# A graph attention layer on one core: the second part's instruction order written by hand, the last tile by column halves, one slot more summed on TensorE

## The chip, the cores and the metric

The kernel runs on one core of a Trainium2 chip. Its engines have queues of their own and meet through semaphores: TensorE (PE, matmuls; its weight loads are listed as PEld), VectorE (DVE), ScalarE (ACT), GpSimd (POOL) and SyncE (SP). SyncE and GpSimd issue the DMAs. The metric is the device time of one execution in microseconds (us). The kernel before was run nine times: median 1314.67 us, from 1309.21 to 1318.92.

## What is computed

`x` is 3327 x 1024 in fp32, `adj` a symmetric 0/1 matrix of 3327 x 3327 with ones on the diagonal, in which a row has some 17 ones on average and 37 at most. The weights are 1024 x 1024. Cut to what matters:

```python
h = jnp.maximum(_layernorm(x), 0.0)
f = h @ Wf + bf
g = h @ Wg + bg
e = relu(f @ g.T)
attention = softmax(where(adj > 0, e, -9e15), axis=1)
out = x + attention @ (h @ W + bW)
```

Only entries with `adj > 0` count, so each row needs the scores of its neighbours alone: `f_i . g_j = (h_i A + v) . h_j + const`, with `A = Wf Wg^T`, and `sum_j p_ij (h_j W + bW) = (sum_j p_ij h_j) W + bW`.

## The kernel before, in words

**First part (to about 270 us; its code is not touched).** It normalises x, writes h to DRAM (`hd`), builds each row's list of neighbours (`pd`), sorts the rows by their number of neighbours, and computes A (`A_sb`). All engines run it in an order written by hand, inside `manual_schedule`.

**Second part.** The sorted rows are 26 tiles of 128. Tile s takes `CAPS[s]` neighbour slots (37, 25, 23 ... 11), and the tiles run in `ORDER`: 24, 15, then 0 to 14, 16 to 23, and 25. The text calls `CAPS[s]` the cap. For a slot k, GpSimd gathers 128 rows of h, one per partition, into a tile `G` (128 x 1024 fp32, 26 buffers). Per tile:

- `fetch`: GpSimd gathers the list `pi` and the tile's own rows `hp`, two tiles ahead. `turned` (L917) transposes `hp` on TensorE, `taken` (L924) copies it to `hT` on ScalarE.
- `third` (L936): q = h A + v in three column thirds, 16 matmuls each, on TensorE, into two banks `ps_q` that ScalarE has filled with v. `emptied` (L946, and L884 by `filled`) copies a third to `q` on ScalarE and fills the bank again. The q of a tile is made two tiles ahead: thirds 0 and 1 behind the earlier tile's combine, the last third inside `project`, and its copy at the next unit's softmax (the list `late`).
- `dot` (L986): a score per slot, one DVE pass over G and q. All three thirds of q must be there.
- `softmax` (L995 to L1011): mask and maximum on DVE (`nm`), the exp on ScalarE (L1002) with its sum l, and, for a second chunk, the correction `al` (L1005) and the scaling of y by it (L1011).
- `combine`: y = sum of p_k G_k. Slot 0 is scaled on ScalarE and becomes y (L1050); the others are either a DVE pass (L1052, "sum" below), or, for the slots that `on_tensor` picks, scaled on ScalarE (L1046) and added on TensorE as 8 transposes that accumulate in PSUM (L1026, `yT_ps`). A slot on TensorE is called a slot on PE below, and m is their number.
- `project`: y itself is added into `yT_ps` the same way, ScalarE copies it to `yT` (L1060), and TensorE multiplies it by W (L1068, 32 matmuls).
- `result` (L1090, L882): ScalarE scales the product by 1/l and fills the banks again; GpSimd adds x by a gather. `finish` (L1102) writes the rows out. For the last tile DVE does it (L1084).

Tiles with more than 16 slots (0 to 14) are done in two chunks: the first of 10 slots (19 for tile 0), all summed on DVE, then the rest, of which m = min(cap - 12, slots - 2) go to TensorE. A one-chunk tile sends cap - 12 there; the two last tiles, 23 and 25, cap - 7; the first two half. A "unit" is a tile's chunk. Each unit of the main loop (L1147 to L1193) runs, in the order of the text: its dots, its softmax, the copy of a last third from `late`, up to three dots of the next unit (`AHEAD`), `finish`, `turned`, `combine`, and, behind a tile's last chunk, `result` of the tile before, `third` 0, its copy, `third` 1, and then `rest` (the copy of third 1, and `project`), which waits until behind the next unit's combine where the next unit is a first chunk.

**What sets the order.** In the second part the queues are not in the order of the text. A planner with a cost model places each engine's instructions. `in_line` chains some of them: the instructions made inside it come behind the last ones noted in `queue["pe"]` and `queue["act"]`. This holds the projections, the transposes, the copies, the exp and the last scaling of a tile in the text's order on TensorE and ScalarE; dots and sums on DVE are placed by the planner.

Of the kernel before, what the change touches and what calls it, by code (L numbers as in the profile page):

```python
# [33 lines left out]
AHEAD = 3  # L34
# [262 lines left out]
def edge_path(ctx: ExitStack, tc: tile.TileContext, x, adj, Wf, bf, Wg, bg, W, bW, out, flag):  # L297
# [563 lines left out]
    queue = {}  # L861

    @contextmanager
    def in_line():
        with ExitStack() as both:
            for ins in queue.values():
                both.enter_context(tc.issue_after(ins.ins))
            yield


# [15 lines left out]

    one = small.tile([P, 1], FP, name="one")
    tc.keep_in_program_order(nc.scalar.activation(one, ident[:, :1], AF.Exp))

    for at in range(2):  # L890
        filled(p_q, "ps_q", vb, QB, 6 + at, True)
        filled(p_o, "ps_o", bWb, CB, at, True)
# [15 lines left out]
    def turned(s):  # L908
        e = st[s]
        e["hT"] = hTpool.tile([P, KD, P], FP, name="hT")  # L910
        e["ps_t"] = []
        for g in range(0, KD, 4):
            ps = p_t.tile([P, 4, P], FP, name="ps_t")
            e["ps_t"].append(ps)
            with in_line():
                for k in range(4):
                    ins = nc.tensor.transpose(ps[:, k, :], e["hp"][:, (g + k) * P : (g + k + 1) * P], ident)  # L917
            queue["pe"] = ins

    def taken(s):  # L920
        e = st[s]
        for g, ps in enumerate(e["ps_t"]):
            with in_line():
                queue["act"] = nc.scalar.copy(e["hT"][:, 4 * g : 4 * g + 4, :], ps)  # L924

    def third(s, i):
# [7 lines left out]
        with in_line():  # L934
            for k in range(KD):
                ins = nc.tensor.matmul(  # L936
                    ps[:, :QB], e["hT"][:, k, :], A_sb[:, k, o : o + QB], start=False, stop=(k == KD - 1),
                    skip_group_check=True,
                )
        queue["pe"] = ins  # L940

    def emptied(s, i):
        e = st[s]
        at = 3 * ORDER.index(s) + i
        with in_line():
            ins = nc.scalar.copy(e["q"][:, i * QB : (i + 1) * QB], e["ps_q"][i][:, :QB])  # L946
            if at + 2 < 3 * NT:
                ins = filled(p_q, "ps_q", vb, QB, at + 2)
        queue["act"] = ins
# [27 lines left out]
    G = {}  # L977

    def dot(s, k, behind=None):
# [5 lines left out]
        with tc.issue_after(behind.ins) if behind else ExitStack():  # L985
            nc.vector.tensor_tensor_reduce(  # L986
                junk, g, e["q"][:, :D], 1.0, e["q"][:, D : D + 1], op0=ALU.mult, op1=ALU.add,
                accum_out=e["sc"][:, k : k + 1],
            )

    def softmax(s, k0, k1, last):
# [5 lines left out]
        nc.vector.tensor_reduce(nm, sc, AX.X, ALU.max, negate=True)  # L997
        if k0:
            nc.vector.tensor_tensor(nm, nm, e["nm"], op=ALU.min)  # L999
        l = small.tile([P, 1], FP, name="l")  # L1000
        with in_line():
            nc.scalar.activation(sc, sc, AF.Exp, bias=nm, accum_out=l)  # L1002
        if k0:
            al = small.tile([P, 1], FP, name="al")
            nc.scalar.activation(al, e["nm"], AF.Exp, bias=nm, scale=-1.0)  # L1005
            nc.vector.scalar_tensor_tensor(l, e["l"], al, l, op0=ALU.mult, op1=ALU.add)
        if last:
            e["rs"] = small.tile([P, 1], FP, name="rs")
            nc.vector.reciprocal(e["rs"], l)
        if k0:  # L1010
            queue["act"] = nc.scalar.activation(e["y"], e["y"], AF.Copy, scale=al)  # L1011
        e["nm"], e["l"] = nm, l

    def on_tensor(s, k0, k1):


        m = min(max(0, CAPS[s] - (7 if s in ORDER[-2:] else 12)), k1 - k0 - 2) if s not in ORDER[:2] else (k1 - k0) // 2
        ks = range(max(k0, 1), k1)
        return [k for i, k in enumerate(ks) if (i + 1) * m // len(ks) > i * m // len(ks)]

    def sum_transposed(e, g, first, last):
# [3 lines left out]
        for c in range(KD):  # L1025
            ins = nc.tensor.matmul(  # L1026
# [210 lines left out]
```

## Time and profile before

| what | value |
|---|---|
| median of 9 runs | 1314.67 us |
| profiled execution | 1314.56 us, span 1312.8 us |
| busy: PE, DVE, ACT, POOL | 1119.6, 1157.4, 609.9, 891.1 us |
| second part from 399 to 1246 us: PE, DVE | 786.9, 793.5 of 847 us |
| dots L986 | 468, 1284 ns each |
| sums L1052 | 275, 1285 ns each |
| scalings for TensorE L1046 | 167, 1142 ns each |
| gathers of G, bytes read over the span | 454; 284 GB/s read and written |

The span runs from the first to the last instruction of one profiled execution; the execution's own time is 1.8 us longer. Busy times are the union of an engine's instructions; matmuls are pipelined, so a busy PE is not at its peak. In a time line a row gives start and duration in us, engine, line, operation, output <- inputs, count, and in brackets how long the engine stood idle before it and what ended that. DVE instructions overlap at their ends: a sum of 1.28 us is followed by the next one 1.2 to 1.3 us after its start.

### The profile page before, as it was taken

The page shows a single profiled execution, that of the slowest core. Times are in us where ns is not written, and L with a number is a line of the kernel's source. Part 1 is how long each engine was busy: PE and PEld are TensorE (multiplying, and loading weights), DVE is VectorE, ACT ScalarE, POOL GpSimd, SP SyncE. Part 2 cuts the span into 40 slices and gives each one's busy share as a digit, 9 for nine tenths or more (in the row PEclk, how much of TensorE's full clock was granted, in tenths as well). Part 3 has the DMA queues.
Part 4 walks back from the last instruction along what each step waited for, and adds up shares of the span by engine and source line. Part 5 has one row for each costly group of instructions (what it writes and reads, how often), then busy time and mean ns, then how long its engine had stood idle before and what let it go on. Part 6 is the DMA issues. An engine that isn't in the chain of part 4 may idle for free.

```text
span 1312.8 us, 14316 instructions
## 1 busy us (share of the span) xinstructions
PE 1119.6 (85%) x4488; PEld 703.8 (54%) x4488; DVE 1157.4 (88%) x2205; ACT 609.9 (46%) x943; POOL 891.1 (68%) x678
## 2 busy tenths in 40 slices
PE   2799962958837999899889998999999899999995
PEld 2566641644615556556655655556555565555553
DVE  6999977687899888999999999999999999999990
ACT  5999976133207345435542454443345433333350
POOL 8999974375675777777667666776665666666611
PEclk9899985987878999899999999999999999999998
DMA  9999995787787998899888898888888788888821
GB/s 372 415 398 403 408 326 184 273 307 259 242 286 241 319 321 285 291 308 310 276 297 276 280 310 291 282 276 288 280 289 273 223 279 290 273 297 273 280 74 50
DMA packets 101802, 374.44 MB, mean 285 GB/s; under 512 B 14747, under 2 KB 18490, under 8 KB 98519
## 3 DMA queue, kind: packets, MB, share of 16 engines
q0 software_dynamic: 80624, 290.96, 66.7%
q1 hardware_dynamic: 21094, 82.49, 16.3%
q8 instruction: 37, 0.61, 0.2%
q14 instruction: 47, 0.39, 0.1%
HBM read 344.11 MB, written 29.30 MB: 284 GB/s over the span
## 4 chain that ended last, share of the span: by engine, by line
DVE 32%; issue 29%; DMA 14%; PE 9%; POOL 7%; ACT 5%; another core or an unknown queue 2%; SPq 0%; POOLq 0%; DVEq 0%; ACTq 0%
DVE G L1052 13%; DMA G<-hd,pi 8%; DVE cand L482 6%; POOL G L356 6%; DVE junk L986 6%; PE yT_ps L1026 4%; PE ps_o L1068 3%; DMA xt<-in_x_dram 3%; PE ps_q L936 2%; ACT G L1046 2%; DVE sc L986 1%; DMA A_sb<-in_L_gnn_Wg_dram 1%; DVE held L493 1%; DMA G<-hd,perm 1%
## 5 line engine op out<-in xcount | busy, mean ns | idle before, releaser
L356 POOL DMA_INDIRECT G<-hd,pi x454 | 535.6, 1180 | 198.5 <-issue 103.6
L986 DVE CUSTOM_DVE_ANT_0 junk<-G,q 128x1024 bf16<-128x1024 f32 x468 | 601.0, 1284 | 33.8 <-DMA G<-hd,pi 15.8
L1052 DVE SCALAR_TENSOR_TENSOR G<-G,sc 128x1024 f32<-128x1024 f32 x275 | 353.4, 1285 | 36.8 <-ACT G L1011 21.4
L1068 PE MATMUL ps_o<-W_sb,yT 128*128 128x512 f32 x832 | 363.8, 595 | 6.3 <-ACT yT L1060 6.3
L936 PE MATMUL ps_q<-A_sb,hT 128*128 128x342 f32 x1152 | 347.3, 455 | 9.6 <-issue 9.5
L936 PEld LDWEIGHTS ps_q<-A_sb,hT 128*128 128x128 f32 x1152 | 216.6, 191 | 119.0 <-issue 17.4
L1026 PE MATMUL yT_ps<-ident,G 128*128 128x128 f32 x1544 | 206.3, 285 | 85.8 <-ACT G L1046 65.4
L1068 PEld LDWEIGHTS ps_o<-W_sb,yT 128*128 128x128 f32 x832 | 157.5, 190 | 200.8 <-issue 188.0
L1026 PEld LDWEIGHTS yT_ps<-ident,G 128*128 128x128 f32 x1544 | 177.4, 146 | 118.1 <-ACT G L1046 80.8
L419 POOL TENSOR_TENSOR r<-r,iotaj 128x1664 f32<-128x1664 f32 (+3 forms) x50 | 183.7, 3712 | 12.2 <-ACT r L412 12.2
L1046 ACT ACTIVATE G<-G,sc 128x1024 f32<-128x1024 f32 x167 | 182.4, 1142 | 0.0
L1002 ACT ACTIVATE sc<-sc,nm 128x10 f32<-128x10 f32 (+11 forms) x41 | 12.5, 305 | 342.5 <-DVE nm L999 252.0
L552 PE MATMUL ps_A<-WgT,WfT 128*128 128x342 f32 x432 | 132.7, 466 | 2.1 <-ACT WfT L547 2.1
L482 DVE MAX8 cand<-r 128x8 f32<-128x208 f32 (+2 forms) x416 | 119.1, 360 | 4.0 <-POOL r L419 3.6
L552 PEld LDWEIGHTS ps_A<-WgT,WfT 128*128 128x128 f32 x432 | 82.9, 195 | 43.5 <-issue 3.9
L946 ACT COPY q<-ps_q 128x342 f32<-128x342 f32 x72 | 31.4, 436 | 158.7 <-PE ps_q L936 123.6
L412 ACT ACTIVATE r<-r 128x3327 f32<-128x3327 int32 (+3 forms) x27 | 77.3, 2863 | 7.8 <-DMA r<-in_adj_dram 7.8
L1102 POOL DMA_INDIRECT out_dram<-res,perm x25 | 32.1, 1284 | 68.1 <-DMA res<-in_x_dram,perm 66.2
L356 POOL DMA_INDIRECT res<-in_x_dram,perm x25 | 43.1, 1723 | 51.1 <-ACT res L1090 42.6
L924 ACT COPY hT<-ps_t 128x512 f32<-128x512 f32 x48 | 25.4, 580 | 75.6 <-PE ps_t L917 75.6
L356 POOL DMA_INDIRECT pi<-pd,perm x26 | 30.9, 1189 | 33.8 <-DMA cd<-cand 17.7
L536 PE MATMUL ps_tr<-ident,A_sb 128*128 128x128 f32 x128 | 23.0, 343 | 26.3 <-DMA A_sb<-in_L_gnn_Wg_dram 23.3
(139 smaller groups left out, 718.5 us busy)
## 6 DMA issues: line engine op xcount, KB each, us to landing
r<-in_adj_dram SPq DMA_DIRECT2D x24, 1663.5 KB, 12.0
xt<-in_x_dram SPq DMA_DIRECT2D x25, 512.0 KB, 12.7
hd<-xt SPq DMA_DIRECT2D x25, 512.0 KB, 10.5
G<-hd,pi POOLq DMA_INDIRECT x454
A_sb<-in_L_gnn_Wg_dram SPq DMA_DIRECT2D x8, 512.0 KB, 17.2
A_sb<-in_L_gnn_Wf_dram SPq DMA_DIRECT2D x8, 512.0 KB, 11.1
W_sb<-in_L_gnn_W_dram POOLq DMA_DIRECT2D x1, 4096.0 KB
cd<-cand SPq DMA_DIRECT2D x25, 64.0 KB, 11.8
```

What stands on the lines that cost most here:

```text
L356: return nc.gpsimd.indirect_dma_start(out=to, out_offset=None, in_=table, in_offset=bass.IndirectOffsetOnAxis(ap=idx, axis=0), **kw,)
L412: nc.scalar.activation(r[:n, b:e], a[:n, b:e], AF.Sign, accum_out=to)
L419: eng.tensor_mul(r[:n, b:e], r[:n, b:e], iotaj[:n, b:e])
L482: nc.vector.max(cands[t][:n, s * 8 : s * 8 + 8], r[:n, s * SW : min(N, (s + 1) * SW)])
L552: nc.tensor.matmul(ps[:, :QB], WfTs[c][:, k, :], WgT[:, k, o : o + QB], start=(k == 0), stop=(k == KD - 1))
L936: ins = nc.tensor.matmul(ps[:, :QB], e["hT"][:, k, :], A_sb[:, k, o : o + QB], start=False, stop=(k == KD - 1), skip_group_check=True,)
L986: nc.vector.tensor_tensor_reduce(junk, g, e["q"][:, :D], 1.0, e["q"][:, D : D + 1], op0=ALU.mult, op1=ALU.add, accum_out=e["sc"][:, k : k ...
L1026: ins = nc.tensor.matmul(e["yT"][:, c, :], g[:, c * P : (c + 1) * P], ident, is_transpose=True, start=(first and c % 4 == 0), stop=(last a ...
L1046: queue["act"] = nc.scalar.activation(g, g, AF.Copy, scale=p)
L1052: e["summed"] = nc.vector.scalar_tensor_tensor(y, g, p, y, op0=ALU.mult, op1=ALU.add)
L1068: ins = nc.tensor.matmul(ps, yT[:, k, :], W_sb[:, k, o * CB : (o + 1) * CB], start=False, stop=(k == KD - 1), skip_group_check=True,)
L1102: ins = nc.gpsimd.indirect_dma_start(out=out[:, :], out_offset=bass.IndirectOffsetOnAxis(ap=perm[:, s : s + 1] if s < N // P else final, a ...
```

## The change

1. The whole second part runs inside `manual_schedule` for ScalarE, VectorE and TensorE: these three take their instructions in the order of the text. `in_line`, `queue` and the other explicit order edges go. GpSimd and SyncE stay with the planner.
2. The text's order is new in places. `softmax` issues the correction `al` ahead of the exp, and the scaling of y right behind it; l and its inverse move to `totalled`, behind the dots that follow. `AHEAD` is 2 instead of 3, from the third unit on. `combine` calls `between` behind each DVE sum, which puts one dot of the next unit there (not in the last tile but one).
3. `on_tensor`: a second chunk of s slots sends min(cap - 11, s - 1) to TensorE instead of min(cap - 12, s - 2): one more in each of the 15 two-chunk tiles, so that DVE sums one slot there. Tile 23 sends 3 instead of 6, tile 25 sends 5 instead of 4.
4. The last tile (25) runs `ended` instead of `combine` and `project`: slot 0 is scaled on DVE, y is summed on DVE by column halves, and each half is transposed, copied and multiplied by its half of W's rows before the next. `result` of tile 23 stands ahead of it in the text.
5. The load of the flag that chooses the dense path moves to behind the last `finish` but one.

Cut to its core:

```diff
-AHEAD = 3
+AHEAD = 2
...
-    def softmax(s, k0, k1, last):
+    def softmax(s, k0, k1):
...
         if k0:
             nc.vector.tensor_tensor(nm, nm, e["nm"], op=ALU.min)
-        l = small.tile([P, 1], FP, name="l")
-        with in_line():
-            nc.scalar.activation(sc, sc, AF.Exp, bias=nm, accum_out=l)
+            e["al"] = small.tile([P, 1], FP, name="al")
+            nc.scalar.activation(e["al"], e["nm"], AF.Exp, bias=nm, scale=-1.0)
+        nc.scalar.activation(sc, sc, AF.Exp, bias=nm, accum_out=l)
         if k0:
-            al = small.tile([P, 1], FP, name="al")
-            nc.scalar.activation(al, e["nm"], AF.Exp, bias=nm, scale=-1.0)
-            nc.vector.scalar_tensor_tensor(l, e["l"], al, l, op0=ALU.mult, op1=ALU.add)
-        if last:
-            e["rs"] = small.tile([P, 1], FP, name="rs")
-            nc.vector.reciprocal(e["rs"], l)
-        if k0:
-            queue["act"] = nc.scalar.activation(e["y"], e["y"], AF.Copy, scale=al)
+            nc.scalar.activation(e["y"], e["y"], AF.Copy, scale=e["al"])
+        else:
+            e["y"] = G[s, 0]
+            if s != ORDER[-1]:
+                nc.scalar.activation(e["y"], e["y"], AF.Copy, scale=e["sc"][:, :1])
...
-        m = min(max(0, CAPS[s] - (7 if s in ORDER[-2:] else 12)), k1 - k0 - 2) if s not in ORDER[:2] else (k1 - k0) // 2
+        if s in ORDER[:2]:
+            m = (k1 - k0) // 2
+        elif s in ORDER[-2:]:
+            m = {ORDER[-2]: 3, ORDER[-1]: 5}[s]
+        else:
+            m = min(max(0, CAPS[s] - (11 if k0 else 12)), k1 - k0 - 1)
...
+                nc.vector.scalar_tensor_tensor(y, g, p, y, op0=ALU.mult, op1=ALU.add)
+                between()
+
+    def ended(s, k1):
...
+        for i, k in enumerate(pe):
+            nc.scalar.activation(G[s, k], G[s, k], AF.Copy, scale=e["sc"][:, k : k + 1])
+            for c in range(KD):
+                transposed_into(e, G[s, k], c, not i and c % 4 == 0, False)
+        for g in range(0, KD, 4):
+            half = slice(g * P, (g + 4) * P)
+            nc.vector.tensor_scalar(y[:, half], y[:, half], e["sc"][:, :1], None, op0=ALU.mult)
...
+            for c in range(g, g + 4):
+                transposed_into(e, y, c, False, c % 4 == 3)
+            nc.scalar.copy(yT[:, g : g + 4, :], e["yT"][:, g : g + 4, :])
+            for o, ps in enumerate(e["o"]):
+                for k in range(g, g + 4):
...
+    with tc.manual_schedule(engines={
+        mybir.EngineType.Activation, mybir.EngineType.DVE, mybir.EngineType.PE
+    }):
...
+            dots(s, range(k0, k1))
...
+            softmax(s, k0, k1)
+            if late:
+                emptied(late.pop(), 2)
+            covered = AHEAD if i > 1 else 0
+            dots(s2, range(a, min(b, a + covered)))
+            totalled(s, k0, last)
...
+            coming = iter(range(a + covered, b) if i > 1 and s != ORDER[-2] else ())
+
+            def between(s2=s2, coming=coming):
+                for k in coming:
+                    dots(s2, [k])
+                    break
+
+            if s == ORDER[-1]:
+                result(ORDER[at - 1])
+                ended(s, k1)
+                done_with.append(ORDER[at - 1])
+                break
+            combine(s, k0, k1, last, ahead, between)
+            if rest:
+                rest()
+                rest = None
+            if last:
+                if at:
+                    result(ORDER[at - 1])
+                    done_with.append(ORDER[at - 1])
+                if ahead is not None:
+                    third(ahead, 0)
+                    emptied(ahead, 0)
+                    third(ahead, 1)
...
+        finish(done_with.pop())
+        bad = nc.values_load(flag[0:1, 0:1], min_val=0, max_val=1 << 20)
+        result(ORDER[-1])
+        finish(ORDER[-1])
```

## The prediction, made before the result was known

> **What bounds the kernel now.** I read the windows by stage first, then VectorE's (DVE's) waits, then the time lines around three hand-overs. The second part runs from about 270 us to the end at 1312.8; from 399 us on it repeats one pattern per row tile, and at 1246 us a tail begins. The windows (columns: busy us of each engine, granted clock, DMA share, GB/s):
>
> ```profile
> core 0: us, PE busy (x) PEld busy (x) DVE busy (x) ACT busy (x) POOL busy (x), PEclk, DMA share, GB/s
> 399.00:1246.00 847.00, 786.89 (x3219) 493.12 (x3220) 793.49 (x1162) 360.99 (x575) 581.42 (x480) 0.99 0.86 285
> 1246.00:1313.00 67.00, 52.27 (x193) 28.27 (x191) 31.26 (x40) 20.96 (x29) 8.98 (x8) 0.92 0.23 64
> ```
>
> DVE has work for 793.5 of 847 us, so it sets the pace, with TensorE (PE) just behind. In the tail DVE has 31 us of 67: PE sets the end there. What DVE lacks in the 847 us is mostly ScalarE (ACT), in the list of its waits (us in total, times, longest):
>
> ```profile
> DVE G L1052 <- ACT G L1011: 21.4, 14, 1.7
> DVE G L1052 <- ACT G L1050: 9.3, 7, 3.1
> DVE l L1006 <- ACT al L1005: 5.8, 9, 0.7
> ```
>
> So 36 us could come back. Why these waits are small is seen where a tile's second chunk (18 slots of the first two-chunk tile, softmax ready at n = 398.97) hands over to the next tile's first chunk. ACT, then DVE:
>
> ```profile
> 417.79 1.16 ACT L1046 ACTIVATE G<-G,sc 128x1024 f32<-128x1024 f32 x1
> 418.85 0.68 ACT L1090 ACTIVATE res<-ps_o,rs 128x512 f32<-128x512 f32 x1
> ...
> 425.60 0.45 ACT L946 COPY q<-ps_q 128x342 f32<-128x342 f32 x1 [4.01 <-PE ps_q L936]
> 426.45 0.30 ACT L1002 ACTIVATE sc<-sc,nm 128x10 f32<-128x10 f32 x1
> 426.88 1.15 ACT L1050 ACTIVATE G<-G,sc 128x1024 f32<-128x1024 f32 x1
> ```
>
> ```profile
> 426.69 1.28 DVE L986 CUSTOM_DVE_ANT_0 junk<-G,q 128x1024 bf16<-128x1024 f32 x1
> 428.06 1.28 DVE L1052 SCALAR_TENSOR_TENSOR G<-G,sc 128x1024 f32<-128x1024 f32 x1
> ```
>
> The next chunk's scores were ready on DVE at 418.8, but its exp ran only at 426.45: ACT first scaled 16 slots for PE, then stood at the copy of q, which waits for PE. DVE lost nothing, because the planned order put seven more dot products (418.7 to 427.9) in front of the first weighted sum. That cover is what I look for in the new order.
>
> **The change, part by part.** Prices, start to start: a dot in a run 1.325 (425.37 to 426.69), a sum in a run 1.31 (three in 3.93), a sum and a dot alternating 2.405; a slot's scaling on ACT 1.05 (13 in 13.63); 8 transposes on PE 0.90 (56 matmuls in 6.28); a third of q 4.7 (two in 9.37); one output projection 13.9.
>
> (1) One slot more on PE in 15 two-chunk tiles: DVE loses one sum each, 1.2 us where it was paired, some 16 to 18 us in all. PE and ACT gain 0.9 and 1.05 each. On PE that is covered (a tile of cap 20 needs 3 x 4.7 + 13.9 + 1.0 + 10 x 0.9 + 0.7 = 38.7 there, below its 42 us); on ACT it lies in the chain above and delays the next exp. GpSimd's gathers stay with the planner: DVE waited 2.0 us for them in all, and a later DVE asks for them later: 0, bounds -2 and +3.
>
> (2) The order by hand, at the second chunk's softmax. It puts two dots of the next tile behind the softmax, as cover. They need that tile's q, whose last third is copied on ACT behind the correction, the exp and the scaling of y: 0.19 + 0.43 + 1.04 + 0.42 issue to issue in the rows at 399.0, so the dots start at n + 2.15. Today DVE lost 0.65 + 1.67 there in ten tiles and 1.2 in four. The cover covers nothing; gain 0.2 in ten, loss 1 in four.
>
> (3) At the next first chunk. From n DVE now does: wait 2.15, two dots 2.65, l and its inverse 0.35, the one sum and a dot 2.45, seven dots 9.3, softmax 0.4, two covering dots 2.65. That is n + 20.0; then the sum stands in the queue, and all later dots behind it. ACT: in three undisturbed tiles the copy of q began 9.02 + 1.05 m after n (19.52 at m = 10, 18.47 at m = 9 twice; m slots on PE), and copy to sum took 2.46 (425.60 to 428.06). So the sum starts at the later of n + 20.0 and n + 11.5 + 1.05 m. With the new m = 17, 14, 12, 11, 10, 10, 9, 9 this is 29.35, 26.2, 24.1, 23.05, 22, 22, 20.95, 20.95, and 20.0 for the other six. Fourteen hand-overs: 308.6. From there to the next second chunk's softmax: nine sums, paired while dots are left, and the rest, with 0.8 of small steps: 27.75, 25.1, 23.8, 22.45 twice, 21.35 twice, 20.25 twice, 19.15 twice, 18.05 three times (caps 25 to 17): 297.2. Together 605.8 against 587.8 today (exps at 399.00 and 986.83): **+18.0**. Counted the other way, as DVE work (10 sums; the pairs that are lost give back 0.235 each, net -9.5) plus waits (14 x 2.15 + 28.6 = 58.7 against 35.5), it is +13.7. I take +16.
>
> (4) Transition to one-chunk tiles. The softmax of the tile of cap 16 comes at n + 25.2 (2.15 + 2.65 + 0.35 + 2.45 + 13 dots 17.2 + 0.4) against 28.9: **-3.7**, since sums that now run there are gone or later.
>
> (5) One-chunk tiles. Here the last third of the next q is on PE behind the previous tile's y. Today's first such tile shows that chain:
>
> ```profile
> 1043.81 1.97 PE L1026 MATMUL yT_ps<-ident,G 128*128 128x128 f32 x8 [5.28 <-DVE G L1052]
> 1045.57 5.43 PE L936 MATMUL ps_q<-A_sb,hT 128*128 128x342 f32 x16
> 1051.04 0.44 ACT L946 COPY q<-ps_q 128x342 f32<-128x342 f32 x1 [0.59 <-PE ps_q L936]
> 1051.51 1.28 DVE L986 CUSTOM_DVE_ANT_0 junk<-G,q 128x1024 bf16<-128x1024 f32 x1 [0.51 <-ACT q L946]
> ```
>
> Today two sums ran at 1048.40 while q was late. In the new order two dots stand before the first sum, so a ring closes: q, 2 dots 2.65, inverse 0.2, 11 sums with a dot between 24.05 + 1.2, y on PE 0.9, third 4.7, copy 0.8 = 34.5 us per tile, whatever its cap. Today the seven periods from 1015.72 to 1245.69 sum to 230.0. New: first Q at n + 2.15, six rings 207.0, and 29.7 from the last Q to the softmax (28.1 to y, a dot 1.2, 0.4): 238.85, **+8.9**. Without the ring, caps 14 and 13 would take 33.2 and 31.9 and all but 1 us of it would go.
>
> (6) Tail. Three slots instead of six on PE in the tile before the last, but its nine sums follow two dots that wait for q (n + 4.8): y at n + 19.45, PE's projection ends at n + 36.2 (today 34.8). Then ACT's queue decides:
>
> ```profile
> 1270.93 4.25 ACT L1046 ACTIVATE G<-G,sc 128x1024 f32<-128x1024 f32 x4
> ...
> 1280.61 0.69 ACT L1090 ACTIVATE res<-ps_o,rs 128x512 f32<-128x512 f32 x1 [4.13 <-PE ps_o L1068]
> 1281.33 0.69 ACT L882 ACTIVATE ps_o<-bWb,l 128x512 f32<-128x512 f32 x1
> ```
>
> Today the last tile's slots were scaled ten us before ACT stood at the result copy; in the new text that copy comes first. So scaling starts 1.55 after the projection, five slots end on PE at 7.8, four transposes 0.45, copy 0.65, half the matmuls 7.0 and the same again: 24.1, against 19.2 today. The halves save nothing, since y is whole before PE gets there (n + 40 against n + 44); the scaling of a half on DVE, not in the trace, lies between 0.24 (a 128x40 form) and 1.28 and is hidden by the same wait. End at n + 60.3 against 53.9: **+6.4**.
>
> (7) Start (270 to 399): 24's and 15's sums run unpaired, but the gathers (POOL waited 7.4 us for a result copy at 333.7) set the first chunk's end: +0.3, bounds -3 and +3. The flag's load moved to the end lies beside 14 us of matmuls: 0, at most 1.
>
> Sum: 0.3 + 16 - 3.7 + 8.9 + 6.4 = +28. The profiled execution took 1314.56 (span 1312.8 and 1.8 around it), 0.1 below the median; so **1342.5 us**.
>
> A rule against my term (3): the Trainium skill, TensorE: Matmul & The Clock Gate, Part 4: PE-mode transpose, says that transposes do not count as PE activity in the way matmuls do and leave the full clock off. Here the clock was 0.73 in 550 to 560, amid transposes, but 1.00 in 560 to 570, and two thirds of q took 9.37 from 561.0 on; by this row the rule adds nothing. By the rule, with its half clock for a 3.4 us window, each of eight handovers would lose 1.7 more, an estimate of +14.
>
> **Rivals.** (A, faster) DVE's waits do vanish and it stays the bound: -35.5 waits, -9.5 work, -9 in one-chunk tiles would be 1260; PE with its 38.7 at cap 20, close to the 39 that DVE's own work would then take, and gathers at 0.86 share leave perhaps two thirds: 1278. For it: DVE is the busiest engine. Against: rows 399.0 to 402 (q behind y on ACT) and 425.60. It decides if the covering dots start within 0.3 us of the maximum. (B, slower by less) sums gain where I see a stall, the ring is broken because y is earlier than I count, only the tail and half of (3) remain: +14, near 1327. (C, much slower) PE restarts slowly after longer idle, as in the tiles at 450 and 499, where the copy of q was 3.4 and 2.1 us late: eight times 2.5, 1362. (D) the order changes, but time doesn't: gains of (1) meet the losses within 4 us.
>
> **Chances.** Forecast 0.58 (1330 to 1356), B 0.17, C 0.07, D 0.05, A 0.13. A measurement here can tell 0.3%, 4 us. Faster 0.13, same 0.05, slower 0.82. Range 1308 to 1362: it leaves out nearly all of A and half of C.
>
> **What would show it.** Right: DVE waits of about 2 us for the copy of q before the first dot after each second chunk's softmax; waits for the scaling of y of 9, 6, 4, 3 us in the first four hand-overs; one-chunk periods near 34.5; ACT scaling the last tile's slots after the last result copy. Wrong: these waits below 0.5 us, or DVE's idle time in the stretch below 40 us.

## The result, and the profile after

The changed kernel takes 1377.9 us (median of 9 runs, 1374.2 to 1385.7), beside 1316.8 for the kernel before in the same runs (27 runs): a ratio of 1.0475, 95% interval 1.0453 to 1.0498. So the change costs 61 us. The forecast was 1342.5, +28, with a range to 1362: the sign was right, the size less than half. The profiled execution has a span of 1378.4 us.

Section 1 of the page after, engines with busy time, share and instructions:

```profile
PE 1137.6 (83%) x4592; PEld 727.2 (53%) x4592; DVE 1146.8 (83%) x2199; ACT 623.7 (45%) x955; POOL 887.5 (64%) x678
```

No engine is busier than 83%. VectorE's work fell by 11 us from before (1157.4), near the 9.5 worked out for the two-chunk tiles, while the span rose by 66: the time went into waiting. The waits of VectorE in the second part say where (us in total, times, longest):

```profile
DVE G L1038 <- ACT G L984: 49.9, 10, 16.9
DVE junk L961 <- ACT q L923: 42.7, 18, 4.5
DVE res L1097 <- PE ps_o L1065: 20.7, 2, 18.0
DVE flag L1132 <- PE ps_t L1131: 18.1, 1, 18.1
DVE G L1038 <- issue: 8.2, 2, 7.2
```

The first line is the first sum of a next first chunk, waiting for the scaling of y (the prediction's part 3). With the fifth, two waits of the same line that the view puts down to no engine, it is 58 us; two waits of 1.0 us belong to the first two tiles, and the other 56 us to ten hand-overs. The second line is the covering dots waiting for q (parts 2 and 5), the third the end of the tail. The fourth is in no part of the prediction.

The longest of these hand-overs on ScalarE, in the timeline after (start, us, engine, line, operation; rows left out are marked):

```profile
418.70 0.69 ACT L872 ACTIVATE ps_o<-bWb,l 128x512 f32<-128x512 f32 x1
430.07 0.45 ACT L923 COPY q<-ps_q 128x342 f32<-128x342 f32 x1 [10.69 <-PE ps_q L915]
...
430.93 0.30 ACT L978 ACTIVATE sc<-sc,nm 128x10 f32<-128x10 f32 x1
...
431.36 1.15 ACT L984 ACTIVATE G<-G,sc 128x1024 f32<-128x1024 f32 x1
```

ScalarE stands for 10.69 us at the copy of q's first third; behind it in its queue are the exp and the scaling of y of the next first chunk, which need nothing from that copy. VectorE's sum starts at 432.54, 16.9 us after the last dot.

The stages of the two profiles; n is the end of the last step of the maximum (`nm`) at a second chunk's softmax, n0 of tile 0 and n14 of tile 14, n16 and n23 the softmaxes of tiles 15 and 23 as in the prediction (where before has no such row, its chain of exps):

| Stage | predicted change | measured after | change |
|---|---|---|---|
| start to n0 | +0.3 | 395.6 | -3.4 |
| two-chunk tiles, n0 to n14 | +16 | 627.7 | +39.9 |
| transition, n14 to the next softmax | -3.7 | 25.1 | -3.8 |
| one-chunk tiles, up to n23 | +8.9 | 257.3 | +27.3, of it 18.1 at the flag |
| tail, n23 to the start of the last result | +6.4 | 59.4 | +5.5 |

The fourth row holds the one wait that is new in kind:

```profile
1287.03 0.06 DVE L1129 MEMSET onesf<- 128x1 f32 x1
1305.21 0.14 DVE L1132 CAST flag<-ps_t 1x1 int32<-1x1 f32 x1 [18.13 <-PE ps_t L1131]
```

and TensorE's timeline beside it:

```profile
1291.16 13.89 PE L1082 MATMUL ps_o<-W_sb,yT 128*128 128x512 f32 x32
1304.98 0.19 PE L1131 MATMUL ps_t<-onesf,bad 128*1 128x1 f32 x2
```

`failed` stands in the text behind tile 22's `project`. TensorE takes its tiny matmul after the last third of q and the whole output projection, and VectorE, in strict order too, holds everything until it can copy the flag.

### The profile page after: what moved, and what is told of

Read it like the earlier page. It is cut to its first block, busy times and chain, and to the rows that moved or that the text cites. A ratio compares the mean times of both kernels' runs of the same rounds, so it can differ in the third digit from the quotient of the medians.

```text
span 1378.4 us, 14499 instructions
## 1 busy us (share of the span) xinstructions
PE 1137.6 (83%) x4592; PEld 727.2 (53%) x4592; DVE 1146.8 (83%) x2199; ACT 623.7 (45%) x955; POOL 887.5 (64%) x678
## 5 line engine op out<-in xcount | busy, mean ns | idle before, releaser
L356 POOL DMA_INDIRECT G<-hd,pi x454 | 528.3, 1164 | 224.0 <-issue 100.8
L1038 DVE SCALAR_TENSOR_TENSOR G<-G,sc 128x1024 f32<-128x1024 f32 x257 | 329.8, 1283 | 59.3 <-ACT G L984 49.9
L1082 PE MATMUL ps_o<-W_sb,yT 128*128 128x512 f32 x800 | 353.0, 599 | 12.7 <-issue 9.3
L915 PE MATMUL ps_q<-A_sb,hT 128*128 128x342 f32 x1152 | 342.5, 453 | 1.1 <-ACT ps_q L874 0.7
L1011 PE MATMUL yT_ps<-ident,G 128*128 128x128 f32 x1648 | 223.0, 293 | 114.4 <-ACT G L1034 74.4
L1011 PEld LDWEIGHTS yT_ps<-ident,G 128*128 128x128 f32 x1648 | 200.0, 152 | 141.4 <-ACT G L1034 84.8
L1082 PEld LDWEIGHTS ps_o<-W_sb,yT 128*128 128x128 f32 x800 | 152.8, 191 | 202.1 <-issue 193.4
L419 POOL TENSOR_TENSOR r<-r,iotaj 128x1664 f32<-128x1664 f32 (+3 forms) x50 | 183.7, 3721 | 11.9 <-ACT r L412 11.9
L1034 ACT ACTIVATE G<-G,sc 128x1024 f32<-128x1024 f32 x175 | 187.3, 1139 | 0.0
L977 ACT ACTIVATE al<-nm 128x1 f32<-128x1 f32 x15 | 4.4, 294 | 294.8 <-DVE nm L975 198.0
L356 POOL DMA_INDIRECT pi<-pd,perm x26 | 27.5, 1058 | 44.8 <-ACT ps_A L791 17.5
L899 PE MATMUL ps_t<-ident,G 128*128 128x128 f32 x192 | 26.7, 285 | 27.3 <-DMA G<-hd,perm 27.3
```

Source lines behind the costliest of these rows:

```text
L356: return nc.gpsimd.indirect_dma_start(out=to, out_offset=None, in_=table, in_offset=bass.IndirectOffsetOnAxis(ap=idx, axis=0), **kw,)
L419: eng.tensor_mul(r[:n, b:e], r[:n, b:e], iotaj[:n, b:e])
L915: nc.tensor.matmul(ps[:, :QB], e["hT"][:, k, :], A_sb[:, k, o : o + QB], start=False, stop=(k == KD - 1), skip_group_check=True,)
L1011: nc.tensor.matmul(e["yT"][:, c, :], g[:, c * P : (c + 1) * P], ident, is_transpose=True, start=first, stop=last, skip_group_check=True,)
L1034: nc.scalar.activation(g, g, AF.Copy, scale=p)
L1038: nc.vector.scalar_tensor_tensor(y, g, p, y, op0=ALU.mult, op1=ALU.add)
```

## The experiments

Runs that went together ran on one chip, and those of the second group (h1_half, h2_warm, e5_ring, e6_tail) on another than all the rest. In the second group the kernel before took 1296.8 us, in all others 1313 to 1322. There n0 to n14 takes 606 us in the changed kernel's order, elsewhere 628 to 633; what makes that difference is taken up below. So each ratio is to before in its own group, and stages are compared within a group.

**e1_flag.** The flag's matmul ahead of the projection.

```diff
                 third(ahead, 1)
+                if at + 2 == NT - 1:
+                    failed()          # without its copy
...
                 if at + 2 == NT - 1:
-                    failed()
+                    nc.vector.tensor_copy(flag[0:1, 0:1], flagged[0][0:1, 0:1])
```

> The failure flag's one-column matmul goes ahead of tile 22's output projection on TensorE; the copy of it stays where it was in VectorE's order. Nothing is left out. My theory: the 18.1 us that VectorE stands still at 1287 us is that copy, waiting behind the projection. It goes; the next two dots then wait some 4.5 us for q instead of 2.0, so 15 to 18 us less than the changed kernel: 1360 to 1363. Rival: the end is set by TensorE's projections in any case (tile 22's ends at 1305 whatever VectorE does), and less than 8 us goes: above 1370.

1368.2 us, ratio 1.0378 (1.0313 to 1.0443). The wait at the flag is 0.2 us. From n14 to n23 16.3 us went (282.4 to 266.1); 4.7 came back in the tail (n23 to the end of the last result, 60.2 to 64.9), where the last tile's dots now wait 7.4 us for q. Net 11.6, between theory and rival, and in the median 9.7, since this run's two-chunk tiles took 4.6 more. The wait was real, but part of it covered another.

**e2_exp.** The first third's copy behind the next first chunk's softmax.

```diff
             softmax(s, k0, k1)
+            if early:
+                emptied(early.pop(), 0)
...
                     third(ahead, 0)
-                    emptied(ahead, 0)
+                    early.append(ahead)   # where the next unit is a first chunk
                     third(ahead, 1)
```

> The copy of the first third of q(ahead) goes behind the next first chunk's softmax on ScalarE, instead of ahead of it; TensorE's order stays. Nothing is left out. My theory: the 56 us that VectorE waits at its first sum of each first chunk are ScalarE standing at that copy with the exp and the scaling of y behind it. Free of it the exp can start at the later of n + 20 and n + 5.9 + 1.05 m, so waits of 5 and 2 us stay at m = 17 and 14 and about none elsewhere: 45 us less, 1333 (1325 to 1345). Rival: TensorE, with 39 us of its own per tile at m = 9, becomes the bound, and its late third of q only moves the wait to the next tile's result copy and scalings: above 1355. Rival of no effect: the sum waits for the scaling of y for another reason, 1378.

1333.2 us, ratio 1.0127 (1.0065 to 1.0189): 45 us less, as the theory had it. VectorE's waits in this run:

```profile
DVE junk L961 <- ACT q L923: 29.5, 12, 4.6
...
DVE G L1038 <- issue: 6.0, 2, 5.0
DVE G L1038 <- ACT G L984: 4.2, 3, 2.6
```

Of the 58 us at these sums 10 are left. n0 to n14 fell from 627.7 to 582.1. Moving one copy in ScalarE's queue takes back 45 of the 61 us that the change costs. The rival, that TensorE takes it back, falls.

**e3_q.** The last third's copy ahead of the second chunk's softmax.

```diff
+            if late and k0:
+                emptied(late.pop(), 2)
             softmax(s, k0, k1)
```

> In second chunks the copy of the next tile's last third of q goes ahead of the softmax's three steps on ScalarE instead of behind them. Nothing is left out. The fourteen waits of 2.02 us at the covering dots vanish in every theory. My theory: in the ten hand-overs where the sum waits for TensorE's third of q, VectorE only comes earlier to that wait, and gains just what ScalarE's scalings start earlier (0.87 us); in the four others it gains all: 10 x 0.87 + 4 x 2.0, some 17 us less than the changed kernel, 1361. Rival: the waits add up one for one, 28 us less: 1350.

1352.6 us, ratio 1.0285 (1.0226 to 1.0344): 25 us less, nearer the rival. But its copies of the first third were also 13 us less late in sum than after's (11.5 against 24.9; late against n + 9.02 + 1.05 m in after, and n + 8.15 + 1.05 m here, where the scalings start 0.87 earlier), and this sum is not constant from run to run (28.0 and 30.1 in c1_after and c2_after below). 28.5 us less from n0 to n14, minus 13, is 15, near the theory's 17. The two are not told apart by this run; that the 2.02 us waits can be had back is.

**e4_share.** TensorE's old share in the new order (`cap - 12`, `slots - 2`).

> The hand-written order with TensorE's old share of the sums in two-chunk tiles (one slot fewer in each of 15). Nothing is left out. My theory: in ten tiles the chain scalings, transposes, third of q sets the next exp, and is shorter by 1.05 us and by some 0.5 to 1 of TensorE's lateness; in five tiles VectorE gets 1.2 us more: 4 to 14 us less than the changed kernel, 1364 to 1374. Rival: VectorE's own work counts (15 x 1.2), 18 us more: 1396. Rival: the lateness of TensorE grows so steeply with the number of slots that it goes by 2 us per tile or more: below 1360.

1372.7 us, ratio 1.0420 (1.0358 to 1.0481), which overlaps the changed kernel's interval. n0 to n14 took 619.1, 8.6 less. So the extra slot is worth nothing in this order, and costs perhaps a few us: the low end of the theory. Both rivals fall.

**b1_share.** The other half of the question: the new share alone, in the kernel before.

```diff
-        m = min(max(0, CAPS[s] - (7 if s in ORDER[-2:] else 12)), k1 - k0 - 2) if ...
+        m = min(max(0, CAPS[s] - (7 if s in ORDER[-2:] else 11 if k0 else 12)),
+                k1 - k0 - (1 if k0 else 2)) if ...
```

> The kernel before with the new share of TensorE alone (one slot more in 15 two-chunk tiles), planner and order as before. Nothing is left out. Theory: VectorE was the bound there and loses 1.2 us per tile, but the covered exp comes 1.05 us later in the eight tiles with most slots: 6 to 14 us faster than before. Rival: the later chain takes it all back (within 4 us of before), or more (slower).

1301.5 us, ratio 0.9840 (0.9805 to 0.9875): 17.9 us faster than before, 1.2 us for each of 15 tiles, more than I had expected. The planner's order covers the later exp: VectorE's waits at its first sums (`G L1052 <- ACT G L1050`) come to 8.9 us, beside 9.3 in before. This part of the change is a gain by itself.

**e5_ring, e6_tail.** In one-chunk tiles no dots ahead of the first sum, and the first two sums unpaired; in the last tile the scalings ahead of the result copies.

```diff
-            covered = AHEAD if i > 1 else 0
+            single = last and not k0 and i > 1
+            covered = AHEAD if i > 1 and not single else 0
...
+            wait = [2 if single else 0]
...
+                if wait[0]:
+                    wait[0] -= 1
+                    return
                 for k in coming:
```

```diff
         for i, k in enumerate(pe):
             nc.scalar.activation(G[s, k], G[s, k], AF.Copy, scale=e["sc"][:, k : k + 1])
+        result(ORDER[-2])
+        for i, k in enumerate(pe):
             for c in range(KD):
...
             if s == ORDER[-1]:
-                result(ORDER[at - 1])
```

> In one-chunk tiles no dot of the next tile stands ahead of the first sum, and the first two sums go without a dot; the rest of the order stays. Nothing is left out. My theory (a ring q, two dots, sums, y, third of q): the ring has 5 us of slack then, the waits for q of 2 to 4.5 us go, and each sum waits some 1.6 us for the exp and the scaling instead: periods of 34.2 at cap 15, 33 at 14, 31.6 at 13, 6 us less in all: 1372. Rival: VectorE's work is the bound as it is (the waits only show where time is to spare), no gain: 1378.

> In the last tile the scalings of its five TensorE slots go ahead of the previous tile's result copies on ScalarE. Nothing is left out. My theory: they then lie beside the projection of the tile before, and the end comes some 5 us earlier: 1373. Rival: the transposes of these slots on TensorE (5 x 0.9 us, behind the projection in any order) are what takes the time, and less than 2 us go: 1376 or more.

Both expectations in us were set against 1378, and the group has its own level (before at 1296.8), so the stages tell. e5_ring: 1348.5 us, ratio 1.0388 (1.0364 to 1.0412). n16 to n23 took 252.7, against 255.9 to 257.4 in the three others of its group; periods are 34.6, 34.6, 34.5, 33.2, 33.3, 31.9, near those worked out, 3 to 5 us less in all where 6 were expected. e6_tail: 1350.2 us, ratio 1.0402 (1.0379 to 1.0425). From n23 to the end of the last result it took 56.2 us, against 59.1 to 62.1: 4 us less than the 60.2 of the changed kernel, where 5 were expected. Both theories hold, a little smaller than expected.

**c1_after, c2_after.** The changed kernel again.

> The changed kernel itself again, beside runs of before on the same chip, since the two groups of runs so far differ in one thing: TensorE's done signals came up to 8 us late in the first group (before: 1316) and on time in the second (before: 1297). Theory: the stretch from the first to the last second-chunk softmax is 606 us where they come on time and 628 where they come late, all else being equal: 1354 or 1378 us, with before at 1297 or 1316. Rival: the lateness belongs to the changed kernel's own order, and comes again whatever before takes: 1378 beside 1297.

> The changed kernel, unchanged, beside the kernel before on one chip. Nothing is left out. Theory: its stretch is 606 us where TensorE's signals are on time and 625 to 633 where they are late; so the order by hand costs 30 to 36 us there in the one case and 36 to 46 in the other, and of the 24 us that the prediction missed in this term some 8 are lateness and some 15 a comparison of an undisturbed chain (605.8) with a disturbed profile (587.8). Rival: the difference to before is 18 us where signals are on time, as predicted, and all the rest is lateness.

1381.3 us (ratio 1.0478, 1.0449 to 1.0507) and 1389.4 (1.0521, 1.0453 to 1.0589), with n0 to n14 at 631.3 and 633.4. Neither fell on a chip like the second group's. There, h2_warm (1353.3 us, ratio 1.0424) stands for the changed kernel, since its edit moved no stage: 56.5 us over before.

**h1_half, h3_half, h2_warm, h4_warm: why is TensorE late?** The prediction's part 3 put the copy of the first third at n + 9.02 + 1.05 m. How many us later it was in tiles 0 to 7 (m = 17, 14, 12, 11, 10, 10, 9, 9):

| Run | 0 | 1 | 2 | 3 | 4 | 5 | 6 | 7 |
|---|---|---|---|---|---|---|---|---|
| changed kernel | 7.6 | 5.3 | 2.7 | 3.0 | 1.1 | 3.3 | 0.8 | 0.1 |
| c1_after | 7.5 | 5.0 | 5.5 | 2.3 | 2.6 | 2.6 | 0.8 | 0.7 |
| c2_after | 5.9 | 3.8 | 7.2 | 3.9 | 2.7 | 3.5 | 1.1 | 1.0 |
| e6_tail (second group) | 0.1 | 0.1 | 0.1 | 0.1 | 0.1 | 0.1 | 0.1 | 0.1 |
| h4_warm | 2.5 | 0.1 | 1.1 | 0.1 | 0.1 | 0.1 | 0.1 | 0.1 |

In the group with before at 1296.8 the formula holds to 0.2 us in every tile; in the others the changed kernel misses it in the first six, by 1.1 to 7.6 us. Two theories for it: L, the DMA engines are full then; K, TensorE's clock starts low after idle time. For L the rows of neighbours were halved, which leaves out half of each row (the edit's core, for the slots that it halves):

```diff
-            st["gathered"] = gather(g, hd[:, :], e["edges"][k])
+            st["gathered"] = gather(g[:, : D // 2], hd.rearrange("n (a b) -> (n a) b", a=2), e["edges"][k])
```

For K TensorE was kept busy with matmuls of 512 columns ahead of a tile's first slot (cut to the core):

```diff
             e["yT"] = p_y.tile([P, KD, P], FP, name="yT_ps")
+            for j in range(warm):    # 10, 12, 5, 7, 6, 4, 4, 2 for tiles 0 to 7
+                nc.tensor.matmul(e["yT"][:, :4, :], ident, A_sb[:, 0, :CB], start=True, stop=True)
```

> The changed kernel with half the bytes gathered: from the third tile on, all slots but each tile's first (and the last tile's) fetch 2 KB rows instead of 4 KB, and the engines read that half twice over, with the same counts and sizes of work (a slot's scaling on ScalarE is two halves). It leaves out half of each neighbour's row, so that its output is another one. Theory L: TensorE's done signals, and at times its issue, come late when the gathers fill the DMA engines (share 0.9 to 1.04). With half the bytes the copy of q's first third starts at n + 9.1 + 1.05 m within 0.5 us in all fourteen hand-overs, and some 20 us go: about 1357. Theory K: TensorE is late because its clock starts at 0.57 to 0.66 after idle time; then the lateness (7.6, 5.3, 2.7, 3.0, 1.1, 3.3 us in the first six) stays, and the time is above 1370.

> The changed kernel with TensorE kept busy: ahead of the first slot's transposes of eight two-chunk tiles stand 10, 12, 5, 7, 6, 4, 4, 2 matmuls of 512 columns into the bank that the transposes then overwrite, which fill most of its idle time there (0.87 us each). Nothing is left out. Theory K (clock): the granted clock stays at 1.00 in the first 10 us of these sums, the lateness of the copy of q's first third goes, and the time falls by some 20 us to about 1357. Theory L (late signals while the DMA engines are full): the clock is higher, the lateness stays, and the time is within 5 us of the changed kernel's 1378.

Both fell into the second group, where there is no lateness to take away. h2_warm raised the clock at the start of tile 1's sums to 1.00, from 0.52 in e5_ring, and left n0 to n14 as it was (605.3 against 606.2 and 606.6). h1_half took 1391.8 us (1.0725, 1.0696 to 1.0755): fewer bytes gained nothing, and ScalarE's two half scalings, 1.36 us per slot instead of 1.05, made the stretch 644.8, 38.6 more. 134 slots times 0.31 is 41.5: what ScalarE takes per slot comes through nearly whole, as the chain of part 3 says. So they were run again:

> Again half the bytes gathered (2 KB of each neighbour's row left out, so another output), since the first such run fell on a chip where TensorE's done signals are on time; there the copy of q's first third came at n + 9.3 + 1.36 m (ScalarE's two half scalings take 1.36 us per slot). Theory L, on a chip where before takes some 1316 and the changed kernel shows lateness of 2 to 8 us in its first six tiles: the full DMA engines are what delays the signals, so with half the bytes the copy still comes at n + 9.3 + 1.36 m within 0.7 us, and the ratio to before is at or below 1.07. Rival: the signals are late for another reason; the copy comes 2 us late or more in at least three of the first six tiles, and the stretch is 655 us or more instead of 645.

> Again TensorE kept busy ahead of the sums of eight tiles, for the same reason. On the chip with signals on time it raised the granted clock at the start of the sums from 0.52 to 1.00 and changed nothing (605 us for the stretch against 606). On a chip with late signals, theory L: the clock rises and the lateness of 2 to 8 us in the first six tiles stays, stretch 625 to 633, 1375 to 1382. Theory K: the lateness goes with the low clock, stretch 606 to 610, 1357.

h3_half: 1409.7 us, ratio 1.0713 (1.0676 to 1.0750). Measured against h1_half, nine of the fourteen copies came 1.4 to 2.7 us late, and n0 to n14 took 664.6, although the DMA engines had room. Tiles 1 to 3, late by 5.0, 5.5 and 2.3 us in c1_after on this chip, were on time, and six of tiles 6 to 13, there 0.8 us late at most, were not. The window of 10 us in tile 0's sums (busy time of PE, PEld, DVE, ACT, POOL, then the granted clock, DMA share, GB/s):

```profile
405.00:415.00 10.00, 8.06 (x61) 6.21 (x58) 7.98 (x14) 9.77 (x15) 6.95 (x7) 1.00 0.68 185
```

Theory L, which was mine, falls as the whole reason; that the bytes have no part in it isn't shown. h4_warm: 1360.8 us, ratio 1.0346 (1.0310 to 1.0382), some 20 us below the changed kernel on this chip (17 by the ratios), with n0 to n14 at 608.7 and the last row of the table. The first 10 us of tiles 1 and 2, in c1_after

```profile
456.00:466.00 10.00, 6.18 (x41) 6.18 (x42) 7.80 (x14) 9.71 (x14) 2.88 (x2) 0.63 0.09 17
512.00:522.00 10.00, 5.97 (x31) 5.98 (x32) 7.77 (x15) 9.50 (x13) 3.51 (x3) 0.53 0.35 96
```

and in h4_warm:

```profile
455.00:465.00 10.00, 10.00 (x61) 7.26 (x60) 7.84 (x13) 9.86 (x14) 2.89 (x3) 1.00 0.11 22
506.00:516.00 10.00, 7.71 (x43) 6.22 (x42) 7.77 (x15) 9.42 (x13) 4.08 (x4) 0.83 0.42 136
```

With TensorE's idle time filled the lateness is nearly gone, and so it is in e7_all below, where TensorE idles 1.6 us or less ahead of tiles 1 to 3 (6.5 to 13.3 in the changed kernel). So theory K's remedy works, but its cause isn't shown: e5_ring, in the second group, starts tile 1's sums at a clock of 0.52, and its copy comes on time; and h3_half idles 11.8 us ahead of tile 1 and is on time there too. Nor is idle time needed. In before, tiles 1 and 2 (n = 449.90 and 499.07) are 4.3 and 3.1 us late by the same formula (m = 13 and 11 there), yet from 440 to 525 us TensorE is never idle for more than 1.4 us, and in tile 1 its clock is full:

```profile
450.00:460.00 10.00, 6.99 (x55) 5.54 (x54) 7.68 (x11) 10.00 (x14) 6.88 (x8) 1.00 0.84 262
460.00:470.00 10.00, 7.41 (x53) 5.47 (x52) 9.75 (x19) 9.31 (x12) 7.18 (x7) 1.00 0.90 318
```

In b4_before they are 4.2 and 3.8 us late, with no idle time above 1.1 us.

**e7_all, e8_all_old, e9_mix.** All five edits (e1, e2, e3, e5, e6), with the new share, the old one, and the new one from cap 19 up.

> All five edits at once: the flag's matmul ahead of the projection, the first-third copy behind the next softmax, the last-third copy ahead of the second chunk's softmax, no dots ahead of the first sum in one-chunk tiles, the last tile's scalings ahead of the result copies. Nothing is left out. Theory: VectorE's order now has no wait of over 2 us in two-chunk tiles, the periods of the run with the first-third copy moved (53.6 down to 37.4) less 2.0 each give 554 us for the stretch, one-chunk tiles give 5 us, the flag 12 to 16, the tail 4: 1277 where TensorE's signals are on time, some 1290 where they are late; faster than before by 1 to 2% in both. Rival: TensorE's own 39 us per tile at m = 9 and the gathers take back half of it: 1300 to 1320.

> The same five edits, with TensorE's old share in two-chunk tiles (one slot fewer in 15). Nothing is left out. Theory: with the waits gone VectorE is the bound, and the slot costs it 1.2 us per tile again: 14 to 18 us slower than all five edits with the new share, and before's level (1291 to 1297 where signals are on time). Rival: TensorE is the bound in two-chunk tiles, and the old share is as fast or faster (0 to -5).

> All five edits, with TensorE's new share in the tiles of cap 19 and more, and its old share in those of 18 and 17. Nothing is left out. Theory: with the waits gone the tiles of cap 18 and 17 are TensorE's (36.3 to 37 us of its work against periods of 35.4 to 36.9), which shows as a backlog in the first two one-chunk tiles (36.9 and 39.7 us with the new share, 34.5 with the old); the mix keeps 3 to 5 us of the gain in the first stretch and loses no backlog: 2 to 6 us faster than all five edits with the new share, ratio to before 0.968 to 0.972. Rival: DVE has the time, no difference: 0.973.

e7_all: 1285.2 us, ratio 0.9730 (0.9704 to 0.9756), 34 us faster than before and 96 faster than the changed kernel in its group. Its waits of VectorE:

```profile
DVE G L1038 <- ACT G L984: 21.9, 13, 6.6
DVE rs L996 <- ACT sc L978: 14.5, 11, 5.5
DVE res L1099 <- PE ps_o L1067: 14.4, 2, 11.7
```

The waits for q have left the list. n0 to n14 is 558.0. But the first one-chunk periods are 36.9 and 39.7, against 34.5 and 34.6 with the old share: in the tiles of cap 18 and 17 TensorE, which by the prediction's count needs 36 to 37 us, is busy for 34.1 to 36.7 us of periods of 35.4 to 36.9, and its backlog lands in these two. So e8_all_old is some 4 us slower at most (1289.1, ratio 0.9777, 0.9748 to 0.9806, which overlaps; 7.8 more from n0 to n14, 7.0 less from there to n23), not 14 to 18. e9_mix takes the backlog away (periods of 34.8 and 35.4) but needs 4.1 more from n0 to n14, and brings nothing (1287.7, 0.9772, 0.9726 to 0.9817). My expectations of both fell.

**b2_before, b4_before.** The kernel before, for its profile.

> The kernel before, unchanged, for its profile. Nothing is left out. Theory: its own stretch of two-chunk tiles (first to last exp of a second chunk, 587.8 us in the profile that the prediction used) holds lateness of TensorE too: where signals are on time the stretch is 570 to 577 us, where they are late 583 to 593. Rival: before hides its lateness behind its other work: 585 to 590 on either chip.

> The kernel before, unchanged, for its profile once more. Nothing is left out. Theory: its stretch of two-chunk tiles is 583 to 593 us where TensorE's signals come late (time 1310 to 1325), and 568 to 577 where they come on time (time 1294 to 1301). Rival: it is 584 to 590 in both, and what before gains on the other chip lies outside of the stretch.

1317.5 and 1315.7 us (ratios 0.9985 and 1.0032, both with 1 in the interval). Its two-chunk stretch is 584.5 and 588.4, where the prediction read 587.8. Both fell on the slower side, so what before spends there when TensorE is on time was not seen.

## Why the prediction was wrong in size

**(1) The slot more on TensorE:** the work moved as said. As a part alone it gives the 16 to 18 us in full (b1_share); in the new order, nothing (e4_share), since VectorE waits there anyway.

**(2) The covering dots behind q's last copy:** right. Fourteen waits of 2.02 us, as worked out (2.15).

**(3) The next first chunk:** the mechanism was right, the term too small: "I take +16", measured +39.9. Sums waited 56 us at ten hand-overs (16.9, 11.9, 7.2, 6.4, 3.5, 5.7 and less) where I had 28.6. The step that failed is the start of the copy of q's first third, n + 9.02 + 1.05 m, which I read from three undisturbed tiles of before and took for every tile; with it the sum starts "at the later of n + 20.0 and n + 11.5 + 1.05 m". In the changed kernel the copy came 7.6, 5.3, 2.7, 3.0, 1.1 and 3.3 us later in the first six tiles, and the stretch took 627.7 us instead of the chain's 605.8. Where TensorE was on time (the second group), it took 605.3 to 606.6: there the chain holds. Rival C, "the copy of q was 3.4 and 2.1 us late", had seen such lateness in before, and at 0.07 got too small a chance. Its numbers are 4.3 and 3.1 us by the prediction's own formula, and the cause that it names, longer idle time, isn't shown (see before's windows above).

So in these profiles 22 of the 24 us that this term missed are TensorE's lateness in the changed kernel (627.7 against 605.8); the other 2 are the step from +18.0 to "I take +16". But before's 587.8, which I subtracted, holds lateness too, and how much of the miss would stand without any can only be estimated. With TensorE late, start and stretch came to -3.4 + 39.9 = 36.5. In the second group the change costs 56.5 us in all; if transition, one-chunk tiles and tail cost 29.0 there as well, 27.5 is left. The forecast was 16.3. So of 20 us missed here some 11 would stand in both, and some 9 are lateness that the new order has and before hadn't; by the medians, in which the change costs 61 us and not the profiles' 66, it is 5 instead of 9.

**(4), (5), (6)** Transition, ring and tail: right, within 1 us for the transition and the tail; the one-chunk tiles took 241.0 in e1_flag, where the flag's wait is gone, against 238.85. e5_ring and e6_tail show that the ring and ScalarE's queue are indeed what these cost.

**(7) The flag:** "lies beside 14 us of matmuls: 0, at most 1". Wrong: 18.1 us, of which 11.6 are net. I had looked at the load that moved to the end, not at the copy and the matmul that stayed where they were in the text. The planner had placed that matmul at 1228.7, 17 us ahead of tile 23's softmax; after, it comes half a us ahead of it; in an order by hand the text is the order, so that each instruction of the part was moved past everything that stands ahead of it. The start (part 7 too) came 3.4 us earlier, just outside its bounds of 3, but n0 lies between 391.6 and 398.2 in the changed kernel's own runs.

The rule on transposes weighed in the prediction (the Trainium skill, TensorE: Matmul & The Clock Gate, Part 4) would have added 14 us by a half clock, an estimate. In the profile after, the clock was low for some of the first 10 us of tile 0's sums (0.57 in 395 to 405) and 1.00 amid transposes (405 to 415); and a full clock changed nothing where TensorE was on time. So that price is not what was missed, though the sum would have come nearer by it.

**What stays open:** what makes TensorE late, what its idle time has to do with it, why on one chip and not on another, and how long before's stretch is on the latter. The traces differ in one more thing. In the second group they hold an event for every instruction that signals to another engine; in all the others some are missing (after has 414 for the 431 instructions of TensorE that signal, 700 for ScalarE's 823, 1034 for VectorE's 1188). Whether the recording of the profile has a part in the lateness wasn't tested.

## What to carry to other kernels

In an order written by hand every wait holds all that stands behind it on its engine: for each instruction that waits for another engine, ask what independent work is queued behind, and move the copy behind that work (45 us here for one line). Instructions that a planner had moved freely, like the flag's, are part of the change even where the diff leaves them untouched. And subtract like from like: a chain of undisturbed tiles (605.8) and a span with disturbances in it (627.7) differ here by more than the 16 us that were forecast.

## What the runs showed of the hardware

TensorE's work and its done signal come apart. In the profile after, TensorE's records in tile 0 are

```profile
418.60 1.04 PE L915 MATMUL ps_q<-A_sb,hT 128*128 128x342 f32 x3
419.92 1.31 PE L915 MATMUL ps_q<-A_sb,hT 128*128 128x342 f32 x4 [0.27 <-issue]
421.38 7.43 PE L915 MATMUL ps_q<-A_sb,hT 128*128 128x342 f32 x25
```

The first third is 16 of these matmuls, so its last ends at 424.2, and ScalarE, which waits for nothing else, starts its copy at 430.07. The trace's signal events of TensorE are at 430.05 for this third, 430.21 for the second (records end 428.80) and 430.37 for the transposes of y behind them (430.35): three signals 0.16 us apart for work that takes 4.6 and 1 us, so it is the signals that are held back rather than all of the work (the profile models the ends of these records). The last slot's signal came 8.4 us behind its record. Those signals of ScalarE and VectorE that the same trace holds come with their records' ends. In before's tile 1, with little idle time, four signals of slots come within 0.28 us (470.43 to 470.71), where a slot's transposes take 0.90. On the second group's chip all of TensorE's signals come with their records' ends:

```profile
416.08 0.69 ACT L872 ACTIVATE ps_o<-bWb,l 128x512 f32<-128x512 f32 x1
419.93 0.45 ACT L923 COPY q<-ps_q 128x342 f32<-128x342 f32 x1 [3.16 <-PE ps_q L915]
```

These are e6_tail's rows for the same tile: a wait of 3.16 us, not 10.69. Matmuls that compute nothing, put into TensorE's idle time, took 17 to 20 us off the changed kernel where its signals are late, and none where they aren't. The Trainium skill (TensorE: Matmul & The Clock Gate, Part 1: The HAM clock gate) says that idle time of a few microseconds drops the clock to half; the windows above agree (0.53 and 0.63 over the 10 us after idle time, 0.83 and 1.00 where it was filled). Why signals are late in some runs and not in others, no run here explains.
